# One product per scan from a stacked dt tile, and the second half's convolution taps as diagonal products, in a kernel of four attention and feed-forward pairs

## The chip, the cores and the metric

The kernel runs on one core of a Trainium2 chip. Its time is the device time of one execution in microseconds, and the median over several executions is compared. The core has five engines that run their own instruction streams in order: PE (TensorE, matrix products into PSUM), DVE (VectorE), ACT (ScalarE), POOL (GpSimd) and SP (SyncE), which here issues nearly all DMAs. They wait for each other by semaphores.

## The reference, cut to what matters

Four layers, each an attention-like part and a feed-forward part with a layer norm after each, on two batch elements of 1024 tokens and 1024 features. The change lies in the third layer's first part, a selective state-space block:

```python
xc = conv_b[None, :, None]
for k in range(K):                       # K = 4 taps along the tokens
    xc = xc + conv_w[None, :, k:k+1] * xp[:, :, k:k+Lq]
xc = jax.nn.silu(xc)
...
dt = jax.nn.softplus(dt + dt_bias[None, :, None])
def step(h, inp):
    x_t, dt_t, B_t, C_t = inp
    dA = jnp.exp(dt_t[..., None] * A)    # 2048 channels x 16 states
    dBx = dt_t[..., None] * B_t[:, None, :] * x_t[..., None]
    h = dA * h + dBx
    y = jnp.einsum('bdn,bn->bd', h, C_t)
    return (h, y)
```

So each of 2048 channels has 16 states, each with its own decay `exp(dt * A)`. Everything is float32.

## The kernel before, in words

`l2_attn` does this block for one batch element. The 2048 channels are 16 tiles `c` of 128 channels on the partitions, and the 1024 tokens are two halves `u` of 512. For each half and tile there is an in-projection (eight 128x512 products into one PSUM bank), the four-tap convolution and a silu (`xcd` in DRAM holds the result), and a gate `z` made by eight more products and a silu.

The first half's in-projections (`l2_in`) run ahead of all else under the planner that the kernel uses outside of hand-ordered stretches. Everything after them is written out by hand (`manual_schedule`, from line 1440): one loop over steps `k` from -23 to the end, in which the order of the code is the order of each engine's stream. Steps 0 to 255 are the scan. Steps -23 to -1 are called the lead-in here.

One step handles 16 states x 8 channels x 2 groups, as a tile `h` of 128 rows by 2 x 512:

- `rows(k+6)`: SP loads dt*x of the channels, each spread over 16 rows (L1260).
- `times_b(k+2)`: POOL multiplies it by B (L1266).
- `decay(k+1, m)`, m = 0, 1: PE spreads dt of eight channels over the 128 rows, by a one-hot matrix `rep`, into PSUM; ACT takes the exp with A as scale, in place (L1274, L1276). The one-hot product is done in the float32r type, once for `hi` (dt rounded) and once for `lo` (the rest), and adds both.
- `scan(k, m)`: DVE's scan along the tokens (L1281). `times_c(k-1)`: DVE multiplies by C (L1292).
- `states(k-2)`, in odd steps: PE adds up the states of two steps (L1303), and once per eight steps D*x by a diagonal matrix (L1301). Every eight steps, `y_out` on DVE takes the finished tile (L1316).

Between these, PE works off a list of fillers, two products a step (three before step -1): in-projections of the second half (`ins(1)`, a unit of eight products at L1332 each), gates (`gates`, L1377), the projection of x, and the first half's out-projection (L1419). In a step `k` the order is: one filler; scan m=0 and decay m=0; the states in odd steps; whatever was put off to this step with `at`; another filler; scan m=1 and decay m=1; the product with C.

A unit of the second half whose last product is in step `now` puts off three things: at `now+1` ACT copies the tile and the history of three tokens to `xp` and makes the first tap with the bias (`l2_x`, L1117 to L1120); at `now+2` DVE adds the three other taps in PSUM (`l2_taps`, L1125); at `now+3` ACT takes the silu (`l2_silu`, L1130) between two loads of its function table. In the scan loop `now+2` is always an odd step, steps 11, 15, 27, 31 and so on to 79; one unit comes at step 0 and five in the lead-in.

dt of a tile is made 16 steps ahead (`l2_dt`): a product (L1212), softplus on ACT and POOL, its product with x on POOL, and in the step 7 later `parts`: ACT copies dt to `hi`, POOL subtracts it to `lo` (L1246, L1247).

Of the kernel before, what the change touches and what calls it, by code (L numbers as in the profile page):

```python
# [8 lines left out]
F = mybir.dt.float32  # L9
I = mybir.dt.int32  # L10
R = mybir.dt.float32r
AF = mybir.ActivationFunctionType
ALU = mybir.AluOpType
# [4 lines left out]
P = 128  # L18
# [5 lines left out]
HALF = 512  # L24
# [3 lines left out]
class Net:  # L28
# [1032 lines left out]
    def l2_attn(self, b, ready, last):  # L1061
        nc, i = self.nc, self.i
# [3 lines left out]
        with (  # L1066
# [4 lines left out]
            cw = self.param(lp, "l2_convw", [P, NCH, 4])  # L1071
            cb = self.param(lp, "l2_convb", [P, NCH])
# [11 lines left out]

            wd = [self.w(i["l2_dtw"][j], NF + 1) for j in range(2)]

            rep = lp.tile([P, 16, P], R, name=self.nm("rep"))
            for j in range(2):
                nc.scalar.copy(rep[:, 8 * j : 8 * j + 8, :].rearrange("p g n -> p (g n)"), self.w(i["l2_rep"][j]))
            hist = lp.tile([P, NCH, 3], F, name=self.nm("hist"))  # L1090
            nc.gpsimd.memset(hist, 0.0)
            hst = lp.tile([P, NCH * N], F, name=self.nm("hst"))
# [1 line left out]
            def tmp(tag, bufs=2, n=HALF):  # L1094
                return tp.tile([P, n], F, tag=tag, bufs=bufs, name=self.nm(tag))
# [8 lines left out]
            px, norms, hl, hs, dA, py, xs = {}, {}, {}, {}, {}, {}, {}  # L1104
# [6 lines left out]
            def at(k, f, *args):  # L1111
                late.setdefault(k, []).append((f, args))

            def l2_x(u, c, p):

                xp = tmp("xp", 1, HALF + 3)
                nc.scalar.copy(xp[:, 0:3], hist[:, c, :])  # L1117
                nc.scalar.copy(xp[:, 3:], p)
                nc.scalar.copy(hist[:, c, :], xp[:, HALF:])
                nc.scalar.activation(p, xp[:, 0:HALF], AF.Identity, scale=cw[:, c, 0:1], bias=cb[:, c : c + 1])  # L1120
                return xp

            def l2_taps(c, p, xp):
                for k in range(1, 4):
                    nc.vector.scalar_tensor_tensor(p, xp[:, k : k + HALF], cw[:, c, k : k + 1], p, ALU.mult, ALU.add)  # L1125

            def l2_silu(u, c, p):
                acc = tmp("xo")
                self.other = True
                nc.scalar.activation(acc, p, AF.Silu)  # L1130
                nc.sync.dma_start(xcd[u][c][:], acc)
                return acc

# [75 lines left out]
            def l2_dt(u, c, k):  # L1209

                p = self.ps()
                nc.tensor.matmul(  # L1212
                    p, wd[c // 8][: NF + 1, (c % 8) * P : (c % 8 + 1) * P], norms[u][0], start=True, stop=True
                )
                xs[u, c] = xc = tmp("xi")
                at(k + 3, nc.sync.dma_start, xc, xcd[u][c][:])
                e, one, lg = tmp("e", 1), tmp("one", 1), tmp("lg", 1)
                dt, dtx = lg, e
                rl = tmp("rl", 1)

                def act1():
                    nc.scalar.activation(rl, p, AF.Relu)
                    nc.scalar.activation(e, p, AF.Abs)
                    nc.scalar.activation(e, e, AF.Exp, scale=-1.0)

                def act2():
                    nc.scalar.activation(one, e, AF.Identity, bias=self.one)
                    nc.scalar.activation(lg, one, AF.Ln)
                    nc.scalar.activation(one, one, AF.Identity, bias=neg)  # L1229

                def pool1():
                    nc.gpsimd.tensor_tensor(e, e, one, ALU.subtract)  # L1232
                    nc.gpsimd.tensor_tensor(lg, lg, e, ALU.add)

                def sum1():
                    nc.gpsimd.tensor_tensor(dt, lg, rl, ALU.add)

                def times_x():
                    nc.gpsimd.tensor_tensor(dtx, dt, xc, ALU.mult)
                    for j in range(4):  # L1240
                        nc.sync.dma_start(dxd[u][c][:, j, :], dtx[32 * j : 32 * j + 32, :])

                def parts():

                    hi, lo = hl[u, c] = [tp.tile([P, HALF], R, tag=t, bufs=2, name=self.nm(t)) for t in ("hi", "lo")]
                    nc.scalar.copy(hi, dt)  # L1246
                    nc.gpsimd.tensor_tensor(lo, dt, hi.bitcast(F), ALU.subtract)  # L1247

                for n, f in ((1, act1), (2, act2), (3, pool1), (4, sum1), (5, times_x), (7, parts)):
                    at(k + n, f)  # L1250


            def of(k):
                return k // SL, k % SL // 8, k % 8 // 2, k % 2
# [15 lines left out]
            def decay(k, m):  # L1270
                u, c, q, jj = of(k)
                dA[k, m] = self.ps()
                for n in range(2):
                    nc.tensor.matmul(dA[k, m], rep[:, 8 * jj + 4 * m + q, :], hl[u, c][n], start=n == 0, stop=n == 1)  # L1274
                g = 16 * c + 4 * q + 2 * jj + m
                nc.scalar.activation(dA[k, m], dA[k, m], AF.Exp, scale=A[:, g : g + 1])  # L1276

# [41 lines left out]
            def ins(u):  # L1319

                def one(u, c):
                    u0 = u * HALF
                    w = {}

                    def load():
                        w["w"] = self.w(i["l2_in"][c])

                    def call(k, now):
                        if k == 0:
                            w["p"] = self.ps()  # L1330
                        p = w["p"]
                        nc.tensor.matmul(  # L1332
                            p, w["w"][:, k * P : (k + 1) * P], self.xcols(k, u0, HALF), start=k == 0, stop=k == KD - 1
                        )
                        if k == KD - 1:
                            def x():
                                w["x"] = l2_x(u, c, p)
                            at(now + 1, x)
                            at(now + 2, lambda: l2_taps(c, p, w["x"]))

                            def s():
                                w["s"] = l2_silu(u, c, p)
                                self.table()
                            at(now + 3, s)
                    return load, [(call, k) for k in range(KD)]
                return [one(u, c) for c in range(NCH)]
# [93 lines left out]
            with self.tc.manual_schedule():  # L1440
# [16 lines left out]
                for k in range(-BEFORE, 2 * SL + 6):  # L1457
                    if -16 <= k < 2 * SL - 16 and k % 8 == 0:
                        l2_dt((k + 16) // SL, (k + 16) % SL // 8, k)
                    if k == SL + 12:  # L1460
                        o = outs(0)
# [5 lines left out]
                    n = 3 if k < -1 else 2  # L1467
# [22 lines left out]
                    for m in range(2):  # L1490
                        if live:
                            scan(k, m)
                        if 0 <= k + 1 < 2 * SL:
                            decay(k + 1, m)
                        if m:
                            break
                        if k % 2 == 1 and 0 <= k - 2 < 2 * SL:
                            states(k - 2)
                        for f, args in late.pop(k, []):
                            f(*args)  # L1500
                        pe(True)
# [366 lines left out]
def layouts(g):  # L1868
    import numpy as np

    c = np.ascontiguousarray
# [14 lines left out]
    o = {"x": c(g("L0_attn_x"))}  # L1886
    w = g("L0_attn_Wqk_w").reshape(P, 2, D)
    bias = g("L0_attn_Wqk_b").reshape(P, 2)
    w = [w[:, 0], w[:, 1], g("L0_attn_Wv_w")]
# [8 lines left out]
    cw = g("L1_attn_conv_w").reshape(3, KD, P, 6, P)  # L1898
# [16 lines left out]
    w = [np.repeat(np.array(m, np.float32), 8) for m in ([1, 1, 0, 0], [1, 0, 1, 0])]  # L1915
    o["l1_part"] = np.stack([1 - w[0], 2 * w[0] - 1, 1 - w[1], 2 * w[1] - 1], 1)

    w = g("L2_attn_in_proj_w").reshape(KD, P, 32, P)
# [4 lines left out]
    w = np.concatenate([g("L2_attn_dt_proj_w").T, np.zeros((32, 2048), np.float32), g("L2_attn_dt_bias")[None]])  # L1923
# [1 line left out]

    o["l2_Alog"] = c(g("L2_attn_A_log").reshape(16, 4, 4, 8, 16).transpose(4, 3, 0, 2, 1).reshape(P, 256))
    eye = np.eye(32, dtype=np.float32).reshape(4, 8, 32)
    w = np.eye(P, dtype=np.float32).reshape(P, 16, 1, 8).repeat(16, 2)
    o["l2_rep"] = c(w.reshape(P, 2, 1024).transpose(1, 0, 2))
    o["l2_sel"] = c(np.tile(eye.transpose(1, 0, 2), (16, 1, 1)))  # L1930
    o["l2_D"] = cols(g("L2_attn_D_param"))
    w = g("L2_attn_out_proj_w").T.reshape(8, 2, P, 2, HALF)
# [38 lines left out]
```

## Time and profile before

| what | time |
|---|---|
| three runs | 5151.29, 5155.25, 5156.01 us; median 5155.25 |
| the profiled execution | 5149.47 us, its span 5146.8 us |
| PE, DVE, ACT, POOL busy, of the span | 95%, 62%, 38%, 39% |
| scan steps of batch element 0 | 1053.5 to about 2008 us |
| scan steps of batch element 1 | 3610.0 to about 4562 us |

The profile gives for each group of instructions its line, the engine, the operation, the tiles that it writes and reads, how often it comes, its busy time and its mean duration, and the idle time of the engine before it with what ended that. Matrix products overlap in the records: a float32 product leaves two records of some 0.6 us that start 0.43 us apart, so on PE starts are compared rather than durations. On the other engines neighbours overlap a little too. "Busy" is an average over stages with different limits, so the view by stretches of time is used beside it.

### The profile page before, as it was taken

To read this page: it belongs to the slowest core of one execution; us is meant where nothing else is said; L and a number is where in the kernel's file an instruction comes from. 1 tells how busy PE (TensorE), PEld (TensorE's weight loads), DVE (VectorE), ACT (ScalarE), POOL (GpSimd) and SP (SyncE) were. 2 spreads that over 40 slices of the span, in tenths; PEclk is the share of its full clock that TensorE was granted. 3 is DMA by queue.
4 is the path that set the end of the run, shared out by engine and by line. 5 is a ranking of instruction groups with operands and counts; after the bars stand their busy time and mean duration, and the time that the engine had idled before them with its cause. 6 is when DMAs were issued, how large, how long until landed. Compare 5 with 4: busy or idle time off the path is not lost. (4 is left out here: it accounts for less than half of the span.)

```text
span 5146.8 us, 51556 instructions
## 1 busy us (share of the span) xinstructions
PE 4867.9 (95%) x17608; PEld 2437.5 (47%) x17608; DVE 3188.3 (62%) x4386; ACT 1942.2 (38%) x3935; POOL 2025.0 (39%) x1195
## 2 busy tenths in 40 slices
PE   8989989999998999999999899899999999999999
PEld 3347645444443444455433576554444444444544
DVE  5453256389999997215364422652999999963153
ACT  2431232377675553001024212324776655520010
POOL 2023120078788884100010220200887888831010
PEclk9999999999999999999999999999999999999999
DMA  2144212477778887201111432113777788861100
GB/s 88 35 160 143 95 48 84 137 207 209 213 203 236 229 244 213 85 33 45 53 63 37 175 116 88 54 59 105 210 210 221 194 239 233 239 206 65 53 21 33
DMA packets 244920, 692.39 MB, mean 135 GB/s; under 512 B 34992, under 2 KB 52528, under 8 KB 244660
## 3 DMA queue, kind: packets, MB, share of 16 engines
q1 hardware_dynamic: 238388, 668.14, 43.6%
q0 software_dynamic: 6272, 20.98, 1.2%
q8 instruction: 140, 2.29, 0.2%
q14 instruction: 120, 0.98, 0.1%
HBM read 600.65 MB, written 86.25 MB: 133 GB/s over the span
## 5 line engine op out<-in xcount | busy, mean ns | idle before, releaser
L1266 POOL TENSOR_TENSOR h<-h,br 128x1024 f32<-128x1024 f32 x512 | 1204.9, 2376 | 33.1 <-DMA h<-dxd 23.2
L1276 ACT ACTIVATE ps<-ps,l_Alog 128x512 f32<-128x512 f32 x1024 | 669.5, 660 | 657.0 <-PE ps L1274 653.6
L1274 PE MATMUL ps<-hi,rep 128*128 128x512 f32 x1024 | 770.1, 752 | 17.1 <-DVE h L1281 17.1
L1281 DVE TENSOR_TENSOR_SCAN h<-ps,hst,h 128x512 f32<-128x512 f32 x512 | 632.9, 1266 | 7.3 <-ACT ps L1276 6.6
L1281 DVE TENSOR_TENSOR_SCAN h<-ps,h 128x512 f32<-128x512 f32 x512 | 604.1, 1207 | 43.2 <-ACT ps L1276 42.5
L1292 DVE TENSOR_TENSOR h<-h,ps 128x1024 f32<-128x1024 f32 x512 | 610.4, 1192 | 0.0
L1377 PE MATMUL ps<-xT,w 128*128 128x512 f32 x1024 | 535.9, 610 | 0.0
L1303 PE MATMUL ps<-h,sel 128*32 128x512 f32 x2048 | 382.1, 610 | 78.3 <-DVE h L1292 78.2
L1586 POOL TENSOR_TENSOR x<-x,row 128x1024 f32<-128x1024 f32 x48 | 112.4, 2352 | 797.8 <-PE ps L130 797.8
L1274 PE MATMUL ps<-lo,rep 128*128 128x512 f32 x1024 | 408.5, 399 | 0.0
L152 DVE TENSOR_TENSOR x<-x,ps 128x512 f32<-128x512 f32 x192 | 128.4, 681 | 438.6 <-PE ps L104 145.7
L1274 PEld LDWEIGHTS ps<-hi,rep 128*128 128x128 f32 x1024 | 196.0, 191 | 299.7 <-issue 208.4
L104 PE MATMUL ps<-xT,w 128*128 128x512 f32 x768 | 336.0, 592 | 0.0
L1274 PEld LDWEIGHTS ps<-lo,rep 128*128 128x128 f32 x1024 | 195.9, 191 | 214.6 <-issue 209.2
L177 ACT ACTIVATE rs<-mv 128x1 f32<-128x1 f32 (+2 forms) x88 | 17.9, 203 | 728.5 <-DVE mv L171 728.3
L104 PE MATMUL ps<-w,xT 128*128 128x512 f32 (+1 forms) x768 | 278.3, 521 | 0.0
L1419 PE MATMUL ps<-w,w 128*128 128x512 f32 x512 | 274.0, 617 | 0.0
L1125 DVE SCALAR_TENSOR_TENSOR ps<-xp,l_convw,ps 128x512 f32<-128x512 f32 x192 | 144.4, 752 | 208.4 <-ACT ps L1120 203.9
L1377 PEld LDWEIGHTS ps<-xT,w 128*128 128x128 f32 x1024 | 185.0, 190 | 161.3 <-issue 132.6
L767 POOL TENSOR_TENSOR s<-s,l1r 128x512 f32<-128x512 f32 x64 | 66.6, 1041 | 489.3 <-DVE l1r L766 483.4
L1332 PE MATMUL ps<-xT,w 128*128 128x512 f32 x512 | 251.0, 600 | 0.0
L1232 POOL TENSOR_TENSOR e<-e,one 128x512 f32<-128x512 f32 x64 | 81.7, 1277 | 414.8 <-ACT one L1229 263.6
(290 smaller groups left out, 7746.5 us busy)
## 6 DMA issues: line engine op xcount, KB each, us to landing
h<-dxd SPq DMA_DIRECT2D x512, 512.0 KB, 6.1
w<-l_in SPq DMA_DIRECT2D x128, 512.0 KB, 6.0
w<-l_out SPq DMA_DIRECT2D x96, 512.0 KB, 5.8
w<-l_conv SPq DMA_DIRECT2D x54, 512.0 KB, 3.7
w<-cvd SPq DMA_DIRECT2D x36, 512.0 KB, 3.3
w<-l_fw SPq DMA_DIRECT2D x32, 512.0 KB, 4.2
xcd<-xo SPq DMA_DIRECT2D x64, 256.0 KB, 2.1
xi<-xcd SPq DMA_DIRECT2D x64, 256.0 KB, 5.3
```

The source lines that it names most:

```text
L104: self.nc.tensor.matmul(out, lhsT, rhs, start=j == 0, stop=j == n - 1)
L152: self.nc.vector.tensor_tensor(xs, xs, p, ALU.add)
L1125: nc.vector.scalar_tensor_tensor(p, xp[:, k : k + HALF], cw[:, c, k : k + 1], p, ALU.mult, ALU.add)
L1266: nc.gpsimd.tensor_tensor(hs[k], hs[k], norms[of(k)[0]][1].unsqueeze(1).to_broadcast([P, 2, HALF]), ALU.mult)
L1274: nc.tensor.matmul(dA[k, m], rep[:, 8 * jj + 4 * m + q, :], hl[u, c][n], start=n == 0, stop=n == 1)
L1276: nc.scalar.activation(dA[k, m], dA[k, m], AF.Exp, scale=A[:, g : g + 1])
L1281: nc.vector.tensor_tensor_scan(hs[k][:, m, :], dA.pop((k, m)), hs[k][:, m, :], hst[:, g : g + 1] if u else 0.0, ALU.mult, ALU.add)
L1292: nc.vector.tensor_tensor(hs[k], hs[k], norms[of(k)[0]][3].unsqueeze(1).to_broadcast([P, 2, HALF]), ALU.mult)
L1303: nc.tensor.matmul(py[u, c][32 * j : 32 * j + 32, :], self.sel[:, q, :], hs[k - 1 + j // 2][:, j % 2, :], start=False, stop=q == 3,)
L1332: nc.tensor.matmul(p, w["w"][:, k * P : (k + 1) * P], self.xcols(k, u0, HALF), start=k == 0, stop=k == KD - 1)
L1377: nc.tensor.matmul(p, w["w"][:, k * P : (k + 1) * P], self.xcols(k, u * HALF, HALF), start=k == 0, stop=k == KD - 1)
L1419: nc.tensor.matmul(p, y[:, cc, t * P : (t + 1) * P], wt[:, cc * HALF : (cc + 1) * HALF], start=c2 == 0 and cc == 0, stop=last,)
```

## The change

Two parts, both in `l2_attn`.

The decay's product: the rows of one tile now hold `hi` of 64 channels and `lo` of the same 64 channels, so that one product with a matrix that has two ones per column adds both. `hl` is a tile of 128 x 2 x 512, one slice for each half of the channels. ACT copies dt to both slices in one instruction, POOL forms `lo`, and one step later two DMAs on SP's queue put `lo` over the half of each slice that is not of its channels. `rep` shrinks from 16 matrices to 8.

The second half's convolution: ACT no longer makes the first tap nor keeps the history there; it makes four 128x128 diagonal matrices `dk` from the identity, with the taps' weights as scale. PE then does four products of these with the shifted `xp`, in the unit's own PSUM bank, at the step at which DVE did the taps. The bias goes into the silu. The first half's convolution stays on DVE.

```diff
-            rep = lp.tile([P, 16, P], R, name=self.nm("rep"))
-            for j in range(2):
-                nc.scalar.copy(rep[:, 8 * j : 8 * j + 8, :].rearrange("p g n -> p (g n)"), self.w(i["l2_rep"][j]))
+            rep = lp.tile([P, 8, P], R, name=self.nm("rep"))
+            nc.scalar.copy(rep.rearrange("p g n -> p (g n)"), self.w(i["l2_rep"]))
...
-            def l2_silu(u, c, p):
+            def l2_silu(u, c, p, bias=0.0):
...
-                nc.scalar.activation(acc, p, AF.Silu)
+                nc.scalar.activation(acc, p, AF.Silu, bias=bias)
...
+                low = [None]
+
                 def parts():
 
-                    hi, lo = hl[u, c] = [tp.tile([P, HALF], R, tag=t, bufs=2, name=self.nm(t)) for t in ("hi", "lo")]
-                    nc.scalar.copy(hi, dt)
-                    nc.gpsimd.tensor_tensor(lo, dt, hi.bitcast(F), ALU.subtract)
-
-                for n, f in ((1, act1), (2, act2), (3, pool1), (4, sum1), (5, times_x), (7, parts)):
+                    hl[u, c] = tp.tile([P, 2, HALF], R, tag="hl", bufs=2, name=self.nm("hl"))
+                    nc.scalar.copy(hl[u, c], dt.unsqueeze(1).to_broadcast([P, 2, HALF]))
+
+                def rest():
+
+                    lo = low[0] = tp.tile([P, HALF], R, tag="lo", bufs=1, name=self.nm("lo"))
+                    nc.gpsimd.tensor_tensor(lo, dt, hl[u, c][:, 0, :].bitcast(F), ALU.subtract)
+
+                def send():
+
+                    lo = low[0]
+                    for j in range(2):
+                        nc.sync.dma_start(
+                            hl[u, c][64 - 64 * j : P - 64 * j, j, :].bitcast(F), lo[64 * j : 64 * j + 64, :].bitcast(F)
+                        )
+
+                for n, f in ((1, act1), (2, act2), (3, pool1), (4, sum1), (5, times_x), (7, parts), (7, rest), (8, send)):
                     at(k + n, f)
...
-                for n in range(2):
-                    nc.tensor.matmul(dA[k, m], rep[:, 8 * jj + 4 * m + q, :], hl[u, c][n], start=n == 0, stop=n == 1)
+                nc.tensor.matmul(dA[k, m], rep[:, 4 * m + q, :], hl[u, c][:, jj, :], start=True, stop=True)
...
                             def x():
-                                w["x"] = l2_x(u, c, p)
+                                xp = w["x"] = tmp("xp", 1, HALF + 3)
+                                nc.scalar.copy(xp[:, 0:3], hist[:, c, :])
+                                nc.scalar.copy(xp[:, 3:], p)
+                                dk = w["d"] = tmp("dk", 1, 4 * P)
+                                for j in range(4):
+                                    nc.scalar.activation(
+                                        dk[:, j * P : (j + 1) * P], self.ident, AF.Identity, scale=cw[:, c, j : j + 1]
+                                    )
                             at(now + 1, x)
-                            at(now + 2, lambda: l2_taps(c, p, w["x"]))
+
+                            def taps():
+                                for j in range(4):
+                                    nc.tensor.matmul(
+                                        p, w["d"][:, j * P : (j + 1) * P], w["x"][:, j : j + HALF],
+                                        start=j == 0, stop=j == 3,
+                                    )
+                            at(now + 2, taps)
 
                             def s():
-                                w["s"] = l2_silu(u, c, p)
+                                w["s"] = l2_silu(u, c, p, cb[:, c : c + 1])
                                 self.table()
                             at(now + 3, s)
```

More of the change, by code (lines that the diff above doesn't have):

```diff
@@ L1927, in layouts @@
     eye = np.eye(32, dtype=np.float32).reshape(4, 8, 32)
-    w = np.eye(P, dtype=np.float32).reshape(P, 16, 1, 8).repeat(16, 2)
-    o["l2_rep"] = c(w.reshape(P, 2, 1024).transpose(1, 0, 2))
+    w = np.eye(64, dtype=np.float32).reshape(64, 8, 1, 8).repeat(16, 2)
+    o["l2_rep"] = np.tile(w.reshape(64, 1024), (2, 1))
     o["l2_sel"] = c(np.tile(eye.transpose(1, 0, 2), (16, 1, 1)))
```

## The prediction

> **What bounds the kernel now.** I read the page's groups first, to find the lines that the change touches. Columns: line, engine, operation, tiles, count | busy us, mean ns | idle before.
>
> ```profile
> L1274 PE MATMUL ps<-hi,rep 128*128 128x512 f32 x1024 | 770.1, 752 | 17.1 <-DVE h L1281 17.1
> L1281 DVE TENSOR_TENSOR_SCAN h<-ps,h 128x512 f32<-128x512 f32 x512 | 604.1, 1207 | 43.2 <-ACT ps L1276 42.5
> L1274 PE MATMUL ps<-lo,rep 128*128 128x512 f32 x1024 | 408.5, 399 | 0.0
> L1125 DVE SCALAR_TENSOR_TENSOR ps<-xp,l_convw,ps 128x512 f32<-128x512 f32 x192 | 144.4, 752 | 208.4 <-ACT ps L1120 203.9
> ```
>
> 1024 `lo` products go; half of the 192 tap instructions (96, the second half's) leave DVE. Nearly no idle stands before the scans, while the taps as a group sit behind 208 us of idle: what a tap is worth depends on its place. So next the stretches of time (us; scan busy (count); clock; DMA share; GB/s), cut every eight steps of the scan loop, for scans alone and then taps alone:
>
> ```profile
> 1118.00:1145.48 27.48, 18.72 (x16) 1.00 0.73 209
> 1145.48:1178.62 33.14, 19.03 (x17) 1.00 0.72 206
> ...
> 1118.00:1145.48 27.48, 0.00 (x0) 1.00 0.73 209
> 1145.48:1178.62 33.14, 4.47 (x6) 1.00 0.72 206
> ```
>
> A block of eight steps takes 27.48 us without taps. That is DVE: two scans 2.25 and the product with C 1.11 start to start, 3.36 a step, times 8, plus one `y_out` of 0.58, is 27.5. With two units' taps (six instructions) it takes 33.14: 2 x 2.22 more of DVE, and 1.08 of waiting for ScalarE. Five such blocks lie in each of the two batch elements (steps 8 to 79, every second one): ten units. An eleventh unit's taps come at step 0. The other five units' taps come before step 0.
>
> What that earlier stretch is bound by, the timeline of PE and the stretch (PE, PEld, DVE, ACT, POOL busy, clock) show:
>
> ```profile
> 1011.76 20.77 PE L1332 MATMUL ps<-xT,w 128*128 128x512 f32 x48
> 1032.37 1.02 PE L1212 MATMUL ps<-dbc,w 97*128 97x512 f32 x2
> ...
> 991.56:1051.73 60.17, 60.17 (x143) 26.51 (x141) 14.88 (x36) 39.87 (x60) 16.04 (x11) 0.97 0.47 139
> ```
>
> 48 records in 20.61 us, start to start, are 0.429 each without a gap, and an fp32 product of 512 columns leaves two records: 0.858 us. Lead-in: PE-bound. Scan loop: DVE-bound, with PE close behind.
>
> **The change, part by part.**
>
> *The lead-in.* Five units x 4 diagonal products x 0.858 = **+17.2 us** per batch element, and the 15 tap instructions that leave DVE were hidden there (14.88 busy in 60). Here a rule is to be weighed. The Trainium skill (Perfetto Trace Analysis, Identifying the Most-Contended Engine) says that matmul busy time misleads and that headroom on TensorE is to be judged by MFU and the share of weight loading. That share is 26.51 / 60.17 = 44%; read so, more than half of PE is free, 3.43 us a unit hide, and the stretch costs 0. The row decides: starts without a gap leave no room. By the rule the whole sum would be 34 us lower.
> Before its products a unit waits for ScalarE: copies 0.1 + 0.6 and four 128x128 `dk` at some 0.30 (the `dg` row, same form: 0.39, next start 0.29 later), 1.9 us, against the old 1.6. PE has four or more fillers (3.4 us) meanwhile, so mostly it is hidden; but the unit at steps -8 to -6 has a silu (3.2) and the dt activations (1.65) ahead of it on ScalarE, 6.9 us against 6 x 0.858 = 5.1. I take **+1.5** (0 to 4).
>
> *The taps in the scan loop.* One unit at steps 39 and 40, in the timelines of PE, DVE and ACT:
>
> ```profile
> 1172.90 1.30 PE L1303 MATMUL ps<-h,sel 128*32 128x512 f32 x8
> 1174.14 1.13 PE L1377 MATMUL ps<-xT,w 128*128 128x512 f32 x2
> 1174.70 0.80 PE L1274 MATMUL ps<-hi,rep 128*128 128x512 f32 x1
> 1175.34 0.39 PE L1274 MATMUL ps<-lo,rep 128*128 128x512 f32 x1
> 1175.57 1.02 PE L1212 MATMUL ps<-dbc,w 97*128 97x512 f32 x2
> ...
> 1173.02 1.21 DVE L1281 TENSOR_TENSOR_SCAN h<-ps,h 128x512 f32<-128x512 f32 x1
> 1174.15 2.31 DVE L1125 SCALAR_TENSOR_TENSOR ps<-xp,l_convw,ps 128x512 f32<-128x512 f32 x3
> 1176.37 1.22 DVE L1281 TENSOR_TENSOR_SCAN h<-ps,h 128x512 f32<-128x512 f32 x1
> ...
> 1175.77 0.66 ACT L1276 ACTIVATE ps<-ps,l_Alog 128x512 f32<-128x512 f32 x1 [1.44 <-PE ps L1274]
> 1178.41 0.66 ACT L1276 ACTIVATE ps<-ps,l_Alog 128x512 f32<-128x512 f32 x1 [0.55 <-PE ps L1274]
> 1179.09 1.28 ACT L1130 ACT_TABLE_LOAD   x1
> 1182.30 0.66 ACT L1276 ACTIVATE ps<-ps,l_Alog 128x512 f32<-128x512 f32 x1
> ```
>
> In odd steps PE reaches the states (L1303) and must wait for the product with C, which ends as the step's first scan begins: whatever lead PE had is gone there. The four tap products stand right behind the states, and the next decay product behind them. Today that decay's exp starts at 1175.77. After: minus `lo` (0.23), plus 3.43, is 1178.97; the scan that needs it can start 0.63 later, at 1179.60. DVE, rid of the taps, gets there at 1174.15 + 1.13 + 1.11 + 1.13 = 1177.53. First wait: 2.07 us.
> Then the next step. PE has the dt product 0.86, a filler 0.86 and a decay 0.23, so the next exp starts at 1180.92. Behind it on ScalarE stands this unit's silu with its two table loads; from 1178.41 to 1182.30, 3.89 us, the second exp waits for that. After: 1184.81, scan 1185.44, while DVE gets there at 1179.60 + 3.38 = 1182.98. Second wait: 2.46. The other unit of a block has no dt product there: 2.07 + 1.60. Pair: 8.2 us of waits for 4.43 of taps removed. PE's shorter decays let the exps ahead of the gates' silu start sooner, which returns about half of the 1.08 wait of ScalarE: -0.5. Net +3.3 a pair, five pairs: **+16.4** per batch element. The unit at step 0 has no states to wait for, but decays just begin: 3.4 against 2.2, and its silu: **+2** (0 to 4).
> A second rule against a row: the skill's back-to-back gap (TensorE: Matmul & The Clock Gate, Back-to-back issue gap) is 216 ns for 512 columns. That fits the fp32r row (`lo`, 0.23 to the next start), not the fp32 one, 0.858. At 4 x 0.216 a burst would lie inside the 1.36 that the scan has to spare without taps (1177.53 less 1175.54 + 0.63) and the lead-in cost 4.3: the sum would be 4.3 - 5 x 4.9 - 1.5, twice, some 43 us gained. The taps are typed fp32, as the fillers are, so I take 0.858.
>
> *The decay products elsewhere.* 16 x 0.229 = 3.7 us of PE less per block, on the engine that is not the bound: DVE's 27.48 (28.45 in the second half, whose scans are 1266 ns) stays. Only where a silu makes ScalarE late (28.67 blocks) about 0.2 returns, seven times: **-1.5**. This is the part that sounds largest, 1024 x 0.229 = 235 us of PE, and it buys little because DVE covers it.
>
> *The stacked tile.* The copy is 128x1024: 1.04 us (the row of L1089) for 0.61, ScalarE being busy 70 to 75%. `lo` on POOL starts 0.43 later; POOL's work in a block is 8 x 2.34 + 5 x 1.3 = 25.3 of 27.5 and it already waits there. The two sends (128 KB each; the nearest rows, 64 KB and 256 KB, land in 3.4 and 2.1) wait on SP for `lo`; queued behind them are the next rows load (L1260) and weight loads. The rows are issued four steps (13.7 us) ahead of use and land in 6.1, and the stacked tile is first read seven steps, 24 us, after: 0 for all this, and if POOL's cover were gone, about 1 us a block (kept for the range). SP also waits for each silu's output, up to 3 us later now; the same lead covers it. Half of `rep`'s loading (4 copies of 1.04 become 2) lay beside PE: 0.
>
> **Sum** per batch element: 17.2 + 1.5 + 16.4 + 2 - 1.5 = 35.6; twice, **+71**. The profiled execution took 5149.5 us (span 5146.8), so 5220.7; the median of the runs is 5155.25, which gives **5226**.
>
> **Rivals.** *A, faster: PE's slack absorbs the taps.* Were PE several decays ahead of DVE, the 3.43 burst would hide, each pair gives back 4.93, with the rest 5 x 4.93 + 1.5 + 2.2 = 28.3 per batch element, against +18.7 in the lead-in: 5155 - 19 = 5136. For it: PE loses 3.7 us a block. Against: the states' wait in every odd step. It decides where a pair's waits fall under about 1.1 us: 5 x (4.43 + 0.5 - 1.1) = 19. I reckon 8.2.
> *B, the silu is not late* (its scan has more lead than I reckoned): only the first wait stays, 4.1 a pair, so pairs come to -0.8 and each batch element to 17.2 + 1.5 - 4 + 2 - 1.5 = +15: 5186.
> *C, POOL or SP becomes the bound* through the later `lo` and the sends: 1 us in each of 64 blocks on top: 5290. Against: POOL idles 0.5 to 4 us at `lo` and at L1232 in most blocks.
>
> **How the numbers follow.** The step as worked out has 0.62, with 5205 to 5250 of its own (step terms +-2 a pair, 0 to 4 twice); B 0.22, A 0.08, C 0.08. The 8-in-10 range leaves out A and the lowest of B below and C above: 5176 to 5260. About 0.2% (10 us) is what a measurement can tell from no change; faster 0.09, same 0.03, slower 0.88.
>
> **What would show it.** Right: 20 more fp32 products before each first scan, which comes some 18 us later; from step 8 to 87 blocks of 31.5 to 32.5 us where 27.5 and 33.1 took turns, with DVE waiting for ScalarE's exp twice a unit, after the products and after the silu; later blocks unchanged at 28.5 to 31.5. Wrong: tap products at 0.23 each; blocks of 27.5 throughout; PE idle in the lead-in; POOL never idle, or scans that wait for POOL.

## The result, and the profile after

The changed kernel takes 5220.93 us in the median (5210.28 to 5227.35), the kernel before 5153.27 beside it: ratio 1.0134, 95% interval 1.0122 to 1.0145. It is slower, by 68 us where 71 were forecast, and lies within the range. The profiled execution took 5227.35 us, the upper end of its runs (span 5225.6), while that of the kernel before (5149.47) lies under its median, so the traces differ by more than the medians do: 78.8 us of span.

The groups of the page after, read as those of before (line, engine, operation, tiles, count | busy us, mean ns | idle before):

```profile
L1286 PE MATMUL ps<-hl,rep 128*128 128x512 f32 x1024 | 761.7, 755 | 21.6 <-DVE h L1293 21.1
L1293 DVE TENSOR_TENSOR_SCAN h<-ps,h 128x512 f32<-128x512 f32 x512 | 609.3, 1214 | 259.3 <-ACT ps L1288 258.5
```

The 1024 `lo` products are gone. The idle time before the scans of the first 512 tokens (steps 0 to 127 of each batch element, the group `h<-ps,h`) has grown from 43.2 to 259.3 us, nearly all of it ended by ACT's exp: DVE was relieved of taps and now waits. The stretches of eight steps, for the scans alone (us; scan busy (count); clock; DMA share; GB/s), two in the zone of the taps and one behind it:

```profile
1140.62:1172.84 32.22, 18.98 (x16) 1.00 0.71 197
1172.84:1204.97 32.13, 19.20 (x16) 1.00 0.79 212
...
1501.76:1530.00 28.24, 18.89 (x16) 1.00 0.83 219
```

Where blocks of 27.48 and 33.1 took turns, all nine between steps 8 and 79 now take some 32.2. The scans take as long as before; only the gaps between them grew. Behind the zone of the taps a block takes 28.24 for 28.67.

The lead-in in PE's timeline after (start, duration):

```profile
1016.03 6.18 PE L1344 MATMUL ps<-xT,w 128*128 128x512 f32 x14
1022.04 3.60 PE L1361 MATMUL ps<-xp,dk 128*128 128x512 f32 x8
1025.48 7.89 PE L1344 MATMUL ps<-xT,w 128*128 128x512 f32 x18
1033.20 3.60 PE L1361 MATMUL ps<-xp,dk 128*128 128x512 f32 x8
```

A unit's four tap products leave eight records and take 3.44 us start to start (1022.04 to 1025.48), in a row of products without a gap on either side. One unit of the scan loop, in the timelines of PE, DVE and ACT, answers to the unit that the prediction worked through (by the count of the scans it is the one of steps 31 and 32, in both traces, not 39 and 40 as written there):

```profile
1201.75 1.05 PE L1315 MATMUL ps<-h,sel 128*32 128x512 f32 x4 [0.74 <-DVE h L1304]
1202.73 3.70 PE L1361 MATMUL ps<-xp,dk 128*128 128x512 f32 x8
...
1206.73 0.80 PE L1286 MATMUL ps<-hl,rep 128*128 128x512 f32 x1
...
1204.97 1.22 DVE L1293 TENSOR_TENSOR_SCAN h<-ps,h 128x512 f32<-128x512 f32 x1
1208.26 1.22 DVE L1293 TENSOR_TENSOR_SCAN h<-ps,h 128x512 f32<-128x512 f32 x1 [2.07 <-ACT ps L1288]
1214.19 1.22 DVE L1293 TENSOR_TENSOR_SCAN h<-ps,h 128x512 f32<-128x512 f32 x1 [2.46 <-ACT ps L1288]
...
1207.57 0.66 ACT L1288 ACTIVATE ps<-ps,l_Alog 128x512 f32<-128x512 f32 x1 [5.18 <-PE ps L1286]
1210.20 1.28 ACT L1129 ACT_TABLE_LOAD   x1
1211.49 0.69 ACT L1129 ACTIVATE xo<-ps,l_convb 128x512 f32<-128x512 f32 x1
1212.20 1.28 ACT L193 ACT_TABLE_LOAD   x1
1213.49 0.66 ACT L1288 ACTIVATE ps<-ps,l_Alog 128x512 f32<-128x512 f32 x1
```

PE comes to the states with no lead (it idles 0.74 us for the product with C), then does the taps, and the decay behind them starts at 1206.73. ACT has stood idle for 5.18 us and starts the exp at 1207.57; the scan waits 2.07. Then the silu with its two table loads stands ahead of the next exp that is late, which starts at 1213.49; the scan waits 2.46. Both numbers are those of the prediction.

Scan starts give the stages of each trace. For batch element 0 (us; the lead-in counts from the gates' first product to the first scan; "steps 96 on" to the last scan):

| kernel | lead-in | steps 0-7 | 8-79 | 80-95 | 96 on |
|---|---|---|---|---|---|
| before | 68.03 | 31.33 | 275.59 | 68.85 | 579.3 |
| after | 86.24 | 33.73 | 289.61 | 75.42 | 575.74 |
| stacking alone | 69.07 | 31.76 | 273.58 | 66.69 | 575.59 |
| taps as products in the lead-in only | 86.23 | 31.75 | 273.97 | 69.11 | 576.22 |
| taps as products in the loop only | 69.07 | 33.72 | 289.56 | 72.12 | 579.04 |
| decay product twice | 86.47 | 34.64 | 298.14 | 74.6 | 582 |
| float32r taps | 73.76 | 31.23 | 267.06 | 71.95 | 576.49 |
| silu three steps later | 86.23 | 35.39 | 277.47 | 72.0 | 575.79 |
| stacking alone, copy later | 69.07 | 30.8 | 272.22 | 73.6 | 575 |
| combination | 69.07 | 31.22 | 263.2 | 74.93 | 574.06 |

Batch element 0 gives 37.6 us of the 78.8 (after less before: 18.2 + 2.4 + 14.0 + 6.6 - 3.6). Batch element 1, read in the same way, gives 36.2 (lead-in 16.9, scan steps 19.3). The remaining 5.0 lie outside these stages.

Of the 18.2, 1.0 goes with the clock and not with the taps. The first lead-in of the kernel before took 68.03 us at a mean granted clock of 0.97; its second one took 69.30, and those of the stacking alone 69.07 and 69.08, all three at 0.95. So lead-ins with product taps are compared with 69.07 below.

### The profile page after: what moved, and what is told of

The parts are those of the page before. It is cut to its first block, busy times and chain, and to the rows that moved or that the text cites. A ratio compares the mean times of both kernels' runs of the same rounds, so it can differ in the third digit from the quotient of the medians.

```text
span 5225.6 us, 49924 instructions
## 1 busy us (share of the span) xinstructions
PE 4883.9 (93%) x16840; PEld 2307.9 (44%) x16840; DVE 3122.4 (60%) x4290; ACT 1972.9 (38%) x3997; POOL 2020.2 (39%) x1195
## 5 line engine op out<-in xcount | busy, mean ns | idle before, releaser
L1286 PE MATMUL ps<-hl,rep 128*128 128x512 f32 x1024 | 761.7, 755 | 21.6 <-DVE h L1293 21.1
L1293 DVE TENSOR_TENSOR_SCAN h<-ps,h 128x512 f32<-128x512 f32 x512 | 609.3, 1214 | 259.3 <-ACT ps L1288 258.5
L1315 PE MATMUL ps<-h,sel 128*32 128x512 f32 x2048 | 503.0, 620 | 129.8 <-DVE h L1304 122.6
L1286 PEld LDWEIGHTS ps<-hl,rep 128*128 128x128 f32 x1024 | 197.3, 194 | 317.9 <-issue 172.9
L1403 PEld LDWEIGHTS ps<-xT,w 128*128 128x128 f32 x1024 | 185.2, 191 | 223.7 <-issue 199.8
L1315 PEld LDWEIGHTS ps<-h,sel 128*32 128x32 f32 x2048 | 70.2, 108 | 464.7 <-DVE h L1304 328.9
L1786 PE MATMUL ps<-w,xT 128*128 128x512 f32 x512 | 227.0, 596 | 0.0
L104 PEld LDWEIGHTS ps<-xT,w 128*128 128x128 f32 x768 | 144.5, 189 | 183.5 <-issue 177.1
```

What stands on the lines that cost most here:

```text
L104: self.nc.tensor.matmul(out, lhsT, rhs, start=j == 0, stop=j == n - 1)
L1286: nc.tensor.matmul(dA[k, m], rep[:, 4 * m + q, :], hl[u, c][:, jj, :], start=True, stop=True)
L1293: nc.vector.tensor_tensor_scan(hs[k][:, m, :], dA.pop((k, m)), hs[k][:, m, :], hst[:, g : g + 1] if u else 0.0, ALU.mult, ALU.add)
L1315: nc.tensor.matmul(py[u, c][32 * j : 32 * j + 32, :], self.sel[:, q, :], hs[k - 1 + j // 2][:, j % 2, :], start=False, stop=q == 3,)
L1403: nc.tensor.matmul(p, w["w"][:, k * P : (k + 1) * P], self.xcols(k, u * HALF, HALF), start=k == 0, stop=k == KD - 1)
L1786: nc.tensor.matmul(p, self.xcols(k, tt * P, P), wt[k][:, ns], start=k == 0, stop=False)
```

## The experiments

My theory: the stacking is worth little, and the taps on PE cost about 17 us per batch element in the lead-in and about as much in the loop, each for its own reason: PE without a gap there, a late exp and then a late silu here. The rivals: PE's slack takes up the taps (A), the silu is not late (B), POOL or SP becomes the bound through `lo` and its sends (C).

**Stacking alone.** The taps, the first tap on ACT and the silu without bias as before:

```diff
-                            at(now + 2, taps)
+                            at(now + 2, lambda: l2_taps(c, p, w["x"]))
```

> The stacked dt tile alone; the second half's taps stay on DVE. Theory (PE is not the bound of the scan loop, DVE is): the lead-in stays at 68 us, blocks with two units' taps 32.6 to 33.1 us and without 27.5, later blocks 28.2; in all 5143 to 5150 us against 5153, a ratio of 0.998 to 0.9995. Rival C (the longer copy, the later lo on POOL and the two sends cost time): some 1 us per block, 5190 or more. Rival A (the freed 235 us of PE are worth much in the loop): below 5130.

Measured: 5142.1 us, ratio 0.9981 [0.9972, 0.999]. So one half of the change is a small gain. Its blocks of eight steps (the same view as above):

```profile
1123.03:1150.50 27.47, 18.82 (x17) 1.00 0.81 215
1150.50:1183.24 32.74, 19.09 (x16) 1.00 0.77 218
1458.81:1487.07 28.26, 18.88 (x17) 1.00 0.88 230
```

A block without taps stays at DVE's 27.47: 3.7 us of PE were taken from it and it did not move. The gain is the 0.4 us wherever ACT made a block late, here 33.14 to 32.74 and 28.67 to 28.26. Rival C falls: it asked for 1 us in each block, and with the later `lo` and the sends in place the 32 blocks together shrank, by 7.5 us in batch element 0 and 1.3 in 1. Some did grow: the first one by 0.43, some behind step 127 by up to 0.6, and that of steps 80 to 87 by 0.5 and 3.0, of which more below. The forecast for this part was right, a little too small.

**Taps as products in the lead-in only.** The product form under a condition, DVE's form otherwise:

```diff
+                            if now + 2 < 0:
...
+                            else:
```

> Stacked dt tile; taps as diagonal products only for the five units of the lead-in, DVE's taps for the eleven units of the scan loop. Theory: lead-in 86 us instead of 68, twice, so 36 us above the stacked tile alone; blocks of the loop as with the stacked tile alone: 5180 to 5187. A lead-in in which PE has headroom (44% of weight loading): no more than 5 us above the stacked tile alone.

Measured: 5182.21 us, 1.006 [1.0044, 1.0075]. The lead-in takes 86.23 for 69.07: 17.16 us, which is five units x four products x 0.858. Nothing is left for the wait for `dk`, nor for rival A in this stage. (Against the stacking alone the median is 40.1 us longer and the trace's span 36.2; the two lead-ins are 34.3 of that.)

**Taps as products in the loop only.** The same condition turned round (`now + 2 >= 0`).

> Stacked dt tile; diagonal products only for the eleven units at step 0 and later, DVE's taps in the lead-in. Theory: lead-in 68 us, block 0 33.7, blocks 8 to 79 32.1 to 32.2 each, so 36 us below the whole change: 5183 to 5190. The two part costs (this and the lead-in's) add up to the whole's. Rival A: below 5150.

Measured: 5186.31 us, 1.007 [1.0054, 1.0085]. The lead-in is back at 69.07 and steps 8 to 79 take 289.56, as in the whole change. The parts add up: 5142.1 + 40.1 + 44.2 = 5226, against 5221 for all.

**The decay product twice.** Each of the two with half the weight, so that PE has as many products as before and everything else of the change stays:

```diff
-            nc.scalar.copy(rep.rearrange("p g n -> p (g n)"), self.w(i["l2_rep"]))
+            nc.scalar.mul(rep.rearrange("p g n -> p (g n)"), self.w(i["l2_rep"]), 0.5)
...
-                nc.tensor.matmul(dA[k, m], rep[:, 4 * m + q, :], hl[u, c][:, jj, :], start=True, stop=True)
+                for n in range(2):
+                    nc.tensor.matmul(dA[k, m], rep[:, 4 * m + q, :], hl[u, c][:, jj, :], start=n == 0, stop=n == 1)
```

> The whole change, but every decay product is done twice with a matrix of halves, so that PE's decay work is what it was before (0.458 us in place of 0.229) and all else is the change's. Theory: blocks without taps from step 96 on go back from 28.2 to 28.7, blocks 8 to 79 rise by some 0.5 to 1 us as the burst after the states is 0.23 longer and the next step's exp 0.46 later: 10 to 25 us above the whole change, 5231 to 5246. If the decay product is off the path everywhere: 5221, the same. If PE were the bound of the loop: 1024 x 0.229 = 235 us more.

Measured: 5253.71 us, 1.0201 [1.0185, 1.0216]; 8 us beyond what I expected. It is 33 us above the whole change, for 235 us of PE work put back: PE does not bound the loop. In the zone of the taps a pair of blocks takes 66.17 for 64.35, and a later block 29.11, more than the 28.67 of the kernel before. Its later block, and the scan that waits in it, with ACT ahead of that:

```profile
1508.74:1537.85 29.11, 18.87 (x17) 1.00 0.79 216
...
1511.48 1.22 DVE L1294 TENSOR_TENSOR_SCAN h<-ps,h 128x512 f32<-128x512 f32 x1 [1.51 <-ACT ps L1289]
...
1505.97 1.03 ACT L1247 CAST hl<-lg 128x1024 fp32r<-128x1024 f32 x1
1507.02 1.28 ACT L1421 ACT_TABLE_LOAD   x1
1508.32 1.15 ACT L1421 ACTIVATE zo<-zo 128x512 f32<-128x512 f32 x2
1509.49 1.28 ACT L193 ACT_TABLE_LOAD   x1
1510.78 0.66 ACT L1289 ACTIVATE ps<-ps,l_Alog 128x512 f32<-128x512 f32 x1
```

The wider copy (1.03 us) stands directly ahead of the gates' silu. It starts the 3.8 us of silu and table loads 0.43 later than a copy of `hi` did, and with a late exp in front the wait is 1.51 where it was 1.08. So the stacking has a cost, too: in such a block it gives 0.85 us by an earlier exp (1.51 to 0.66 in the changed kernel) and takes 0.43 by the wider copy (1.08 to 1.51); the 0.42 that stays is the gain seen, 28.67 to 28.24. I had put the copy at 0.

**float32r taps.** The diagonal products in the type of the decay products; this rounds the taps' inputs, and is for the time alone:

```diff
-                                xp = w["x"] = tmp("xp", 1, HALF + 3)
+                                xp = w["x"] = tmp("xp", 1, HALF + 3).bitcast(R)
...
-                                dk = w["d"] = tmp("dk", 1, 4 * P)
+                                dk = w["d"] = tmp("dk", 1, 4 * P).bitcast(R)
```

> The whole change with the tap products in the float32r type: 4 x 0.229 = 0.92 us a unit in place of 3.43, and nothing else changed (dk and xp are rounded by ACT as it writes them). Theory (the length of the burst behind the states makes the first wait and the later start of the silu's exp makes the second): lead-in 69.1 + 4.6 = 73.7; no first wait, second wait 2.0 and 1.2, so a pair of blocks takes 27.5 + 27.5 + 3.2 + 0.5 = 58.7 instead of 64.4; in all 5125 to 5142. If not the length but the presence of the products, their wait for dk or ScalarE's work were the cause: blocks of 31 to 32 and above 5190.

Measured: 5141.69 us, 0.9984 [0.9975, 0.9993]. The lead-in loses 12.5 of its 17.2 us. The scans of a pair of blocks that wait over 1 us, in DVE's timeline:

```profile
1125.81 1.22 DVE L1293 TENSOR_TENSOR_SCAN h<-ps,h 128x512 f32<-128x512 f32 x1 [2.14 <-ACT ps L1288]
...
1169.48 1.22 DVE L1293 TENSOR_TENSOR_SCAN h<-ps,h 128x512 f32<-128x512 f32 x1 [1.02 <-ACT ps L1288]
```

In the changed kernel such a pair has four:

```profile
1143.91 1.22 DVE L1293 TENSOR_TENSOR_SCAN h<-ps,h 128x512 f32<-128x512 f32 x1 [2.07 <-ACT ps L1288]
1149.83 1.22 DVE L1293 TENSOR_TENSOR_SCAN h<-ps,h 128x512 f32<-128x512 f32 x1 [2.46 <-ACT ps L1288]
...
1190.94 1.22 DVE L1293 TENSOR_TENSOR_SCAN h<-ps,h 128x512 f32<-128x512 f32 x1 [1.79 <-ACT ps L1288]
1196.00 1.22 DVE L1293 TENSOR_TENSOR_SCAN h<-ps,h 128x512 f32<-128x512 f32 x1 [1.59 <-ACT ps L1288]
```

The waits of 2.07 and 1.79 behind the products are gone; what is left (2.14 and 1.02) comes with the silu. Both kernels have two smaller ones beside these, 0.66 for the gates' silu and 0.16. So the length of the burst, 3.43 us, makes the first wait of a unit. Rival A was in part a question of length: a burst of 0.9 us makes no wait of its own in the loop.

The silu's waits depend little on the burst: of 2.46 and 1.59, 2.14 and 1.02 stay. In the kernel before, the exp behind this silu starts at 1182.30 (the prediction shows the line), is done 0.63 later, and the scan that needs it, the second of these two, starts at 1183.11 without a wait:

```profile
1181.98 2.33 DVE L1281 TENSOR_TENSOR_SCAN h<-ps,h 128x512 f32<-128x512 f32 x2
```

DVE comes there with 0.18 us to spare, two steps behind the taps (1174.15, also shown there), on which it spent 2.2 us, and without a gap since. Without the taps it would come 2.2 us sooner and wait 2.0 for an exp that the silu and its table loads hold back; 2.14 was measured. So the 43 us of gain that the prediction worked out for short products, with no waits left, is not what they give: the pair falls to 59.36, 1.25 below the 60.61 of before, not 4.93.

The result is no better than stacking alone: steps 8 to 79 take 6.5 and 7.3 us less than there in the two batch elements, but the lead-in pays 4.7, and the stretch of steps 80 to 95 takes 5.3 and 3.3 us more.

**Silu three steps later.** Only where no later work of the block needs it at once:

```diff
-                            at(now + 3, s)
+                            at(now + (3 if c >= 14 else 6), s)
```

> The whole change with the second half's silus three steps later (now+6, an odd step; units 14 and 15 as they were), so that the silu isn't behind an exp that the burst has made late. Theory: the first waits stay (2.07 a unit), most of the second go: a pair of blocks 59.6 to 61.5 instead of 64.4, four or five pairs a batch element, 25 to 45 us less in all: 5176 to 5196. Rival: the second wait has another cause (PE's banks, or exps that are late anyway) and moves along: 5215 or more.

Measured: 5195.89 us, 1.0089 [1.0074, 1.0105]. A pair takes 61.35 for 64.35 (the unit at step 0 loses by it: 35.39 for 33.73). In this kernel the same scans are:

```profile
1138.27 1.22 DVE L1293 TENSOR_TENSOR_SCAN h<-ps,h 128x512 f32<-128x512 f32 x1 [2.07 <-ACT ps L1288]
1153.57 1.22 DVE L1293 TENSOR_TENSOR_SCAN h<-ps,h 128x512 f32<-128x512 f32 x1 [1.16 <-ACT ps L1288]
...
1183.99 1.22 DVE L1293 TENSOR_TENSOR_SCAN h<-ps,h 128x512 f32<-128x512 f32 x1 [1.81 <-ACT ps L1288]
```

Now the waits behind the products stay (2.07, 1.81), and of the silu's (2.46, 1.59) one of 1.16 is left at its new place. The two waits of a unit thus have two causes: shorter products take away the one, a later silu most of the other. Rival B, a silu that is not late, comes near this kernel, where a pair costs 0.74 more than the 60.61 of before, and not the changed one, where it costs 3.7.

**Stacking alone, copy later.** To get back the 0.43 of the wider copy, one step later, behind the gates' silu:

```diff
-                ... (7, parts), (7, rest), (8, send)):
+                ... (8, parts), (8, rest), (9, send)):
```

> The stacked dt tile alone (taps on DVE), with the copy to the stacked tile, lo and the sends one step later, so that the copy of 1.04 us no longer stands on ACT right ahead of the gates' silu. Theory (the double-decay run left 29.1 where the kernel before has 28.7, and the copy is 0.43 longer): blocks from step 96 to 127 fall from 28.2 to 27.6, blocks with taps by 0.3 to 0.6; 8 to 14 us less than with the stacked tile alone, 5128 to 5136. If ACT's place for the copy is of no account: 5142.

Measured: 5138.14 us, 0.9972 [0.9961, 0.9982]; 2 us short of the gain, and not clear of the stacking alone, whose interval overlaps. The blocks tell more. Two blocks in the zone of the taps, and one behind it:

```profile
1116.38:1144.49 28.11, 18.85 (x17) 1.00 0.76 204
1144.49:1176.44 31.95, 18.93 (x16) 1.00 0.83 230
1457.73:1485.21 27.48, 18.71 (x17) 1.00 0.97 246
```

The late block fell to DVE's own 27.48, as expected, and blocks with taps to 31.95; but the blocks without taps rose from 27.47 to 28.11, where the copy met another silu. And the block of steps 80 to 87 took 45.39 in one batch element and 36.66 in the other. Neither of the two steps tried suits all blocks, so the next kernel chooses by block.

**The combination.** Stacking; taps on DVE in the lead-in, where PE has no gap, and as float32r products in the loop; the copy at step 7 where at step 8 it would meet a convolution's silu, and at 8 elsewhere. The taps' inputs are rounded here too, so this is also for the time alone:

```diff
+                d = 7 if 0 <= k < 80 and k // 8 % 2 else 8
+                ... (d, parts), (d, rest), (d + 1, send)):
```

> A try for the best: stacked tile; DVE's taps in the lead-in; float32r tap products for the units of the loop; the copy later except in blocks with taps. Theory: lead-in 69, pairs of blocks 58.2 to 58.7, blocks 96 to 127 at 27.6: 5108 to 5125. Rival A in a weak form (short products are still worth nothing on PE): 5130 or more.

Measured: 5127.9 us (5124.98 to 5131.92), 0.9954 [0.994, 0.9967]. It is faster than the kernel before and than the changed one, though 3 us short of what I expected. Steps 8 to 79 take 263.2 us, 12.4 fewer than before, and later blocks 27.48; the block of steps 80 to 87 takes 46.2 for 37.9 of before. There PE and then DVE wait:

```profile
1362.29 2.02 PE L1136 MATMUL ps<-w,wx 128*96 128x512 f32 x2 [3.86 <-DMA w<-xcd]
...
1370.37 1.22 DVE L1294 TENSOR_TENSOR_SCAN h<-ps,h 128x512 f32<-128x512 f32 x1 [3.61 <-ACT ps L1289]
...
1380.77 1.71 DVE L180 TENSOR_TENSOR rsq<-rr 128x12 f32<-128x12 f32 x1 [0.52 <-ACT rr L178]
1382.52 2.26 DVE L181 TENSOR_TENSOR rsq<-rsq,ss 128x12 f32<-128x12 f32 x1
1384.82 2.27 DVE L182 TENSOR_SCALAR rsq<-rsq 128x12 f32<-128x12 f32 x1
1387.11 0.17 DVE L183 TENSOR_TENSOR rr<-rr,rsq 128x12 f32<-128x12 f32 x1
```

The projection of x needs the last unit's silu back from DRAM (`w<-xcd`), and PE waits for it; the decays queued behind that product in PE's order are late, and the scan with them. Then the norm's four operations take 6.4 us, for 4.3 at this place in the kernel before. What the loop gains is paid back in part in this stretch.

## Why the prediction was right

*The bound of each stage.* PE without a gap in the lead-in, DVE in the loop: both held. Two runs show it by what did not happen: 3.7 us of PE less per block left a 27.47 block at 27.47, and each tap product added to the lead-in came out in full.

*The lead-in* was given +17.2 and +1.5. Lead-ins with the tap products take 17.16 us more than those without, to the second decimal the product of the prediction. The wait for `dk` (0 to 4, taken as 1.5) measured 0: PE's fillers cover ACT there. That the trace's 18.2 of batch element 0 comes near 18.7 is luck, as its other 1.0 goes with the clock. The share of weight loading (the Trainium skill, Perfetto Trace Analysis, Identifying the Most-Contended Engine), by which most of this would have hidden, misleads in this stage, whose weight loads are busy 44% of the time; the page names MFU beside it, which the prediction did not work out. Starts without a gap decided.

*The loop pairs* were given +3.3 each. The trace has 64.35 for 60.61: +3.7. The first unit's two waits are exact (2.07 and 2.46); the second's were put at 2.07 + 1.60 and are 0.16 + 1.79 + 1.59. The rest is of one kind: each of the waits costs about 0.1 us more than its idle time, since neighbours on DVE overlap by that much when they do not wait (the scan at 1208.26 comes 2.16 after the 1206.10 at which it would have started, with 2.07 of idle time). The waits of the sum left out this overlap.

*The later blocks* were given -1.5. The four blocks of steps 96 to 127 gave 0.4 to 0.75 each, 2.0 in all, more than assumed. Of the blocks behind them the plain ones stayed at 28.45, and the longer ones moved either way by up to 1.2 us, which makes -3.6 and -0.1 of the two batch elements; what moves these I did not find out. The stacked copy, taken as free, is a part of this balance, as the doubled decay product showed. Step 0's unit was given +2 and measured +2.4, of which 0.43 come with the stacking alone and 2.0 with the taps.

*What the sum did not have* is the stretch of steps 80 to 95, where the last unit meets the norm and the projection of x. With one more pair as worked out it should have grown by about 4.7 in its first block; it grew by 8.0 and 4.5 there in the two batch elements, and gave back 1.4 and 1.6 in its second block. Two things differ between the two: PE's wait for the transfer of the silu's output, 4.04 us in the first and 0.87 in the second, and the norm's four operations, 5.8 and 4.3 us. The wait in the first:

```profile
1413.25 2.02 PE L1136 MATMUL ps<-w,wx 128*96 128x512 f32 x2 [4.04 <-DMA w<-xcd]
```

The kernel before has no such wait. I had written that the lead of four steps covers a silu that comes up to 3 us later. That lead is the one of the rows loads; this load is needed at once, and the silu starts 6.5 us after step 80 begins, for 1.8 before. But a late silu is not the whole cause, for the stacking alone has the wait too (3.44 and 2.25), with its silu as early as in the kernel before, 1.5 us after step 80 begins:

```profile
1376.01 1.85 PE L1136 MATMUL ps<-w,wx 128*96 128x512 f32 x2 [3.44 <-DMA w<-xcd]
```

What the stacking adds there are the two sends of `lo`, which go out on SP's queue just ahead of the silu's output. In its batch element 1 that output lands 6.7 us after its issue, 0.4 us behind the second send; in the kernel before it took 3.6. The prediction had put the sends at 0. The order of the landings fits a delay by the sends, but no run moved them alone, so this cause is argued and not shown.

*The float32 price.* 0.858 us a product, not the 0.216 of the Trainium skill (TensorE: Matmul & The Clock Gate, Back-to-back issue gap), which the page gives for an isolated product of 512 columns, with some 0.131 for a sustained stream, and without a type: the taps in float32 and in float32r differ by 12.47 us over 20 products in the lead-in, 0.62 each, and 0.858 - 0.229 is 0.63. The 0.216 is near float32r's 0.229 and a quarter of float32's price, and the type alone decides whether the change is slower: with float32r taps it measures 0.9984.

The forecast misses the median by 5 us, and the trace by 8 the other way (71 against 78.8), of which 5.0 lie outside the stages of the table. The mechanism of both stages was right; that the total came so near is partly luck, as errors cancel. Steps 8 to 95 were given 16.4 and took 20.6 and 17.0, the wait for `dk` was given 1.5 and took nothing, and the steps from 96 on, given -1.5, returned 3.6 in one batch element and 0.1 in the other.

## What to carry to other kernels

Before moving work onto an engine, ask in each stage whether it has gaps there, and in what units the burst comes: four products of 0.858 us cost their full length in the stage without gaps and a late exp in the other, while the same four at 0.23 hid. Ask also what the work that goes away was covering: the taps' 2.2 us on DVE hid a silu with its table loads, 3.3 us, on ACT, and with the taps gone DVE waits for it even where the products are short. Work taken from an engine that is not the bound (235 us of TensorE here) returns only what it shortens ahead of the late instruction, and a wider instruction on another engine can take half of that back (0.43 of 0.85 us here).

## What the runs showed of the hardware that was not expected

Short DVE instructions can take thirteen times their time. In the norm of the second half, the operations on 128x12 elements take 0.17 us in the lead-in, when POOL does nothing, and up to 2.26 us in the loop. In the changed kernel, DVE and then POOL:

```profile
1430.38 0.17 DVE L180 TENSOR_TENSOR rsq<-rr 128x12 f32<-128x12 f32 x1 [0.52 <-ACT rr L178]
1430.59 1.13 DVE L181 TENSOR_TENSOR rsq<-rsq,ss 128x12 f32<-128x12 f32 x1
1431.75 2.26 DVE L182 TENSOR_SCALAR rsq<-rsq 128x12 f32<-128x12 f32 x1
1434.05 2.26 DVE L183 TENSOR_TENSOR rr<-rr,rsq 128x12 f32<-128x12 f32 x1
...
1430.41 1.27 POOL L1238 TENSOR_TENSOR e<-lg,xi 128x512 f32<-128x512 f32 x1 [8.57 <-DMA w<-l_in]
1431.65 4.63 POOL L1279 TENSOR_TENSOR h<-h,br 128x1024 f32<-128x1024 f32 x2
```

POOL's product ends at 1431.68 and its two multiplies at 1433.98 and 1436.28; the three slow DVE operations end at 1431.72, 1434.01 and 1436.31. Each lasts until the POOL instruction beside it is done, while scans and the products with C, which have an operand in PSUM, keep their 1.2 us beside the same multiplies. This fits what the Trainium skill says (Trainium Architecture — The Big Picture, What this means for kernel authors): VectorE and GpSimd share a port pair under an exclusive lock, not by splitting bandwidth. Some traces hold the other case by accident: in the stacking alone, batch element 0, POOL stands idle through the same norm in the same loop, and the four operations take 0.17 us each.

```profile
1394.05 0.17 DVE L181 TENSOR_TENSOR rsq<-rsq,ss 128x12 f32<-128x12 f32 x1
...
1394.71 1.26 POOL L1238 TENSOR_TENSOR e<-lg,xi 128x512 f32<-128x512 f32 x1 [11.99 <-DVE rr L183]
```

So the stretching comes with POOL's work; that a lock makes it is the page's account, which no run here tests by itself. In the combination the four take 6.4 us at that place instead of 0.7, so a norm within such a loop has a price that its size doesn't tell.
